# Graph attention layer on one core: k's low half kept beside zeros, tile 1 of seven heads transposed by DMA, low halves and copies recorded one step later

## The chip, the core and the metric

The kernel runs on one core of a Trainium2 chip. A core has five engines that work side by side, each through its own list of instructions in order: TensorE (PE, matrix products, with its weight loads PEld), VectorE (DVE), ScalarE (ACT), GpSimd (POOL) and SyncE (SP). SP computes nothing here; it issues most DMA transfers, in order, and one that waits holds up those behind it. The engines tell each other through semaphores. The matrix unit reads from SBUF, 128 partitions of on-chip memory, and writes into PSUM, eight banks of 128x512 floats. The metric is the time of one execution in microseconds. Before the change three runs gave 286.29, 286.67 and 287.81 us, so the median is 286.67.

## What is computed

Input x has 384 rows (nodes) of 1024 features. With H = 16 heads of width 64, cut to what matters:

```
h    = relu(layernorm(x))
q, k, v = h @ wq.T + bq, h @ wk.T + bk, h @ wv.T + bv
q2, k2, v2 = q @ wiq.T + biq, k @ wik.T + bik, v @ wiv.T + biv     # per head 384 x 64
mask = -inf, and softplus(edge weight of its type) where an edge is; the diagonal filled
attn = softmax(q2 @ k2.T / 8 + mask)                              # 16 heads, 384 x 384
y    = x + (attn @ v2) @ wo.T + bo
```

The products are kept close to float32 by splitting every operand into a high half (rounded to the type that PE reads fast) and a low half (what the rounding left). A product then takes three matmuls: high by high, high by low, low by high.

## The kernel before

**Stages.** A weight matrix comes in 8 chunks of 128x1024. A chunk is loaded by SP (`load`, line 70), its high half is made by ACT (`split_hi`, lines 90 and 94) and its low half by DVE or POOL (`split_lo`, lines 101 and 103). `mm3` (lines 432 to 435) issues the three matmuls of a product. The first 150 us hold the layer norm, the projections v and q, the product iv, the projection k, and on POOL and DVE the mask: 51 indirect DMAs of POOL write edge values into tables in DRAM (line 290), which come back and are merged into the tile `ma`. In that stage `extra_v(m)` does POOL and DVE work of the mask after chunk m of v, and `residual` loads the output bias into a tile named `bot`.

**The attention loop.** From about 150 us on, one loop of 60 steps i (line 945) interleaves everything that is left, and this hand-written order sets the order on every engine. A tile i = 3h + t is rows t*128 to t*128+127 of the scores of head h. A pair p is two heads, 2p and 2p+1, whose q and k rows come from one chunk each of wiq and wik.

- Step i: PE makes the scores of tile i (`do_S`, line 844), two matmuls of 384 columns. DVE adds the mask and takes the row minimum of tile i-1 (`do_ttr`, line 850), ACT takes the exponential of tile i-2 (line 854), DVE the reciprocal of the row sum of tile i-3 (line 867). There are two PSUM banks for scores, so the scores of tile i can only be written when DVE has read tile i-2.
- The probabilities have to be transposed before they meet v2. Tile t = 0 goes by DMA: DVE scales the reciprocal (line 869), ACT writes the high half (`do_high`, line 877) into a plane buffer, a step later DVE writes the low half (`do_low`, line 881) and SP issues a DMA transpose of both (`do_turn`, line 885). Tiles t = 1 and 2 go through PE: POOL multiplies by the reciprocal (line 871), PE does three 128x128 transposes per tile (`turn_mm`, line 891) in step 3h+7, a step later ACT (line 898) and DVE (line 899) copy high and low halves out of PSUM (`do_pt`). Three plane buffers lie in a spare part of the tile `pt`.
- Every six steps, `av_mm` (line 909) multiplies a pair's transposed probabilities with v2, 18 matmuls.
- Between those, `fill` gives out the matmuls of the q2 and k2 chunks (`fill_qk`) and later of the output product (`fill_o`), about 2.6 products of three matmuls per step. It runs ahead: 28 products are given out before step 0 (PRE), and a pair's chunks end about five steps before its first scores.
- `qk_head(w)` runs when chunk w begins, every three steps. It evacuates the chunk before (`qk_done`), makes the high half of chunk w+2, and loads chunk w+5. A function put into the list `later` runs in the next step, right after that step's `do_ttr`.

**q2 and k2 of a pair** (`qk_done`). `evac` writes the high half by ACT (line 443) and the low half by DVE (line 444) into the tile `nat`. For q, four copies by DMA put high and low half of a head above each other (64 rows each) into the tile `qs`. For k, four copies of 64 rows put high and low half of a head into both row halves of the tile `ks`. The first score matmul then multiplies q's high and low rows with k's high half, the second both with k's low half.

**Output scale.** `o_scale` (line 643) needs a maximum over all partitions: PE transposes a column (line 142), and DVE reads it in the next instructions (line 124).

Of the kernel before, what the change touches and what calls it, by code (L numbers as in the profile page):

```python
# [26 lines left out]
def gnn_kernel(ctx: ExitStack, tc: tile.TileContext, x, edges, erows, etw, wq, wk, wv, wiq, wik, wiv, wo,  # L27
# [6 lines left out]
    nc = tc.nc  # L34
# [40 lines left out]
    def split_hi(w, dst=None, dve=False):  # L75
        if w >= NCH:
            return
        if dst is None:
            t = wpool.tile([128, 2, D], F32R, tag="whl", name="whl", bufs=4)
            dst = t.rearrange("p a n -> p (a n)")  # L80
        sc = weight_scale(w)
        if sc is not None:
            dst = dst.bitcast(F16)
        whl[w] = dst[:, 0:D], dst[:, D:2 * D]
        hi = whl[w][0]
        if sc is not None:
            if dve:
                nc.vector.tensor_scalar(hi, raw[w], sc, None, op0=OP.mult)
            else:
                nc.scalar.activation(hi, raw[w], AF.Copy, scale=sc)  # L90
        elif dve:
            nc.vector.tensor_copy(hi, raw[w])
        else:
            nc.scalar.activation(hi, raw[w], AF.Copy)  # L94

    def split_lo(w, eng=None):
        if w < NCH:
            hi, lo = whl[w]
# [32 lines left out]
    def bound_of(w):  # L131
        return ((0, t_v, u_v), (1, t_iv, u_iv), (0, t_q, u_q), (1, t_iq, u_iq), (2, t_o, u_o))[BOUNDS[w]]
# [308 lines left out]

    def evac(ps, hi, lo, bias):
        nc.scalar.activation(hi, ps[:, :N], AF.Identity, bias=bias)
        nc.vector.scalar_tensor_tensor(lo, ps[:, :N], bias, hi.bitcast(F32), op0=OP.add, op1=OP.subtract)

    def evac_row(ps, hi, lo, bias):
        f = work.tile([128, N], F32, tag="e", name="f", bufs=EB)
# [49 lines left out]
    def proj(src, dst, bidx, extra=None):  # L497
        nonlocal w
        for m in range(8):
# [26 lines left out]
                extra(m)  # L526
            w += 1

    def extra_v(m):
        detect(m)  # L530

    def detect(s):

        if s == 0:
            softplus_c()
            mask_values()
        if s < NTAB:
# [14 lines left out]
    def residual(k):  # L552

        if k == 0:
            t = work.tile([128, 2, 2, N], F32R, tag="ks", name="bot")
            bob["b"] = t.bitcast(F32).rearrange("p a k n -> p (a k n)")[:, 0:D]
            nc.sync.dma_start(bob["b"], bo.partition_broadcast(128))
        if 1 <= k < 4:
            nc.sync.dma_start(xb[k - 1], x[(k - 1) * 128:k * 128, :])

    def residual_add(i):
        y = res[:, i // 2, i % 2 * 512:i % 2 * 512 + 512]
        nc.gpsimd.tensor_tensor(y, y, bob["b"][:, i % 2 * 512:i % 2 * 512 + 512], OP.add)

    nde = [0]

# [74 lines left out]
            nc.vector.tensor_scalar(ma[:, j, :], ma[:, j, :], u_c, -3.0e38, op0=OP.mult, op1=OP.max)  # L641

    def o_scale():
        bound(W0 + 5)
        nc.vector.tensor_tensor(t_out, t_out, t_o, OP.mult)

    def v2_evac(i):
        t, h = divmod(i, 2)
# [33 lines left out]
    def qk_done(w):  # L682
        n, p = chunks[w]
        q2 = nc.scalar if p == 0 else nc.sync
        nat = work.tile([128, 2, N], F32R, tag="nat", name="nat", bufs=2)
        evac(gps[w], nat[:, 0, :], nat[:, 1, :], bias_q[:, p:p + 1] if n == "iq" else bc[:, 32 + p:33 + p])
        nf = nat.bitcast(F32)
        if n == "iq":
            qs = work.tile([128, 2, N], F32R, tag="qs", name="qs")
            qf = qs.bitcast(F32)  # L690
            copies = [(nc.sync, qf[0:64, 0, :], nf[0:64, 0, :]), (q2, qf[64:128, 0, :], nf[0:64, 1, :]),
                      (nc.sync, qf[0:64, 1, :], nf[64:128, 1, :]), (q2, qf[64:128, 1, :], nf[64:128, 0, :])]
            stacks["q", p] = qs
        else:
            ks = work.tile([128, 2, 2, N], F32R, tag="ks", name="ks")
            kf = ks.bitcast(F32)
            copies = [(q2 if r else nc.sync, kf[r * 64:(r + 1) * 64, o, :, :], nf[o * 64:(o + 1) * 64, :, :])
                      for o in range(2) for r in range(2)]
            stacks["k", p] = ks
        for q, a, b in copies:  # L700
            issue = lambda q=q, a=a, b=b: q.dma_start(a, b)
            if q is nc.scalar:
                issues.append(issue)
            else:
                issue()

    tasks, later = [], []

# [10 lines left out]
    def qk_head(w):  # L719
        if pendq:  # L720
            pendq.pop(0)()
        if 0 < w - W0 < NTAB:
            mask_select(w - W0)
        split_hi(w + 2)
        while issues:
            issues.pop(0)()
        eng = nc.gpsimd if (w + 2) % 2 == PAR else None
        if w + 2 >= WO:
            later.append(lambda: later.append(lambda: split_lo(w + 2)))
        elif eng is None and now[0] >= 0:  # L730
            later.append(lambda: split_lo(w + 2))
        else:
            split_lo(w + 2, eng)
        load(w + 5)
        scan_sum(w)
        if w == W0:
            mask_select(0)
        if w == W0 + NTAB - 1:
            mask_scale()
        bound_max(w)  # L740
        if w == W0 + 6:
            o_scale()
# [64 lines left out]
    def fill_o():  # L807
# [15 lines left out]
        while todo:  # L823
# [8 lines left out]
            omm(*OT[a], k)  # L832
            yield 4

    st_ps, es, sts, tps, avs, aof = {}, {}, {}, {}, {}, {}
    S = 48

    def do_S(i):
        h, t = divmod(i, 3)
        p, o = divmod(h, 2)  # L840
        qs, ks = stacks["q", p], stacks["k", p]
        ps = st_ps[i] = bank("s")
        for s in range(2):
            nc.tensor.matmul(ps[:, :N], qs[:, o, t * 128:(t + 1) * 128], ks[:, o, s, :], start=(s == 0), stop=(s == 1))  # L844

    def do_ttr(i):
        t = i % 3
# [7 lines left out]

    ptv, plv = [], []

    def pt_setup():
        for _ in range(2):
            f = work.tile([128, 2, NT, N], F32, tag="pt", name="pt").rearrange("p a k n -> p (a k n)").bitcast(F16)  # L860
            ptv.extend(f[:, j * 6 * N:(j + 1) * 6 * N].rearrange("p (c n) -> p c n", c=6) for j in range(2))
        f = ptv.pop()
        plv.extend(f[:, 2 * j:2 * j + 2, :] for j in range(3))

    def do_norm(i):
        s = sts[i]
        nc.vector.reciprocal(s[:, 2:3], s[:, 1:2])  # L867
        if i % 3 in DT:
            nc.vector.tensor_scalar(s[:, 2:3], s[:, 2:3], PSC, None, op0=OP.mult)
        else:  # L870
            nc.gpsimd.tensor_tensor(es[i], es[i], s[:, 2:3].to_broadcast([128, N]), OP.mult)  # L871

    planes = {}

    def do_high(i):
        planes[i] = plv[i // 3 % 3]
        nc.scalar.activation(planes[i][:, 0, :], es[i], AF.Copy, scale=sts[i][:, 2:3])  # L877

    def do_low(i):
# [59 lines left out]
    t_at, a_at = {}, {}  # L939
    for h in range(16):  # L940
        for t in (1, 2):
            t_at.setdefault(3 * h + 7 if h < 15 else 3 * h + 5 + t, []).append(3 * h + t)
        if h % 2:
            a_at[3 * h + 10 if h < 15 else 3 * h + 9] = h // 2
    for i in range(S + 12):
        now[0] = i
        r = RATE if len(gens) == 2 else RATE_O if i < S else RATE_E
        fill(r / 2)
        if i < S:
            do_S(i)  # L950
        fill(r / 2)
        if 0 <= i - 1 < S:
            do_ttr(i - 1)
        run_later()
        if 0 <= i - 4 < S and (i - 4) % 3 in DT:
            do_low(i - 4)
        if 0 <= i - 2 < S:
            do_exp(i - 2)
        if 0 <= i - 3 < S:
            do_norm(i - 3)  # L960
            if (i - 3) % 3 in DT:
# [12 lines left out]
        if 0 <= i - 4 < S and (i - 4) % 3 in DT:  # L974
# [64 lines left out]
```

## Time and profile before

| what | value |
|---|---|
| median of three runs | 286.67 us |
| the profiled execution | 286.41 us |
| its span from first to last instruction | 284.7 us |
| granted TensorE clock | 0.999 |
| PE busy | 278.8 us (98%) |
| DVE busy | 214.3 us (75%) |
| ACT busy | 195.4 us (69%) |
| POOL busy | 142.5 us (50%) |
| DMA moved | 66.67 MB |
| transposes on PE | 96 |
| DMA transposes | 16 |
| copies into ks | 32 of 192 KB |

How to read it: the profile shows one execution. The 1.7 us between its time and its span lie outside the recorded instructions. A group's line in the tables gives line, engine, operation, tile written <- tiles read, shape, count, then busy time and mean length of one, then the engine's idle time just before and what ended it. Matmuls overlap each other in the array, so the length of one is not what it adds; what it adds is the distance from its start to the start of the next.

### The profile page before, as it was taken

How to read it: one execution, taken by the hardware profiler on the slowest of the kernel's cores; microseconds unless marked ns; L12 is line 12 of the kernel's file. 1: busy time of each engine (PE TensorE's matmuls, PEld its weight loads, DVE VectorE, ACT ScalarE, POOL GpSimd, SP SyncE). 2: the span in 40 equal slices, each digit the busy share in tenths (PEclk: the TensorE clock that was granted, in tenths of full speed). 3: DMA queues.
4: the chain of work that ended last, by engine and by line, in shares of the span. 5: the costliest groups of instructions: out<-in, count | busy, mean ns of one | idle time of the engine just before them, and what ended most of it. 6: DMA issues, size and time to landing. Idle time of an engine off the chain costs nothing.

```text
span 284.7 us, 5105 instructions
## 1 busy us (share of the span) xinstructions
PE 278.8 (98%) x1663; PEld 222.4 (78%) x1663; DVE 214.3 (75%) x534; ACT 195.4 (69%) x379; POOL 142.5 (50%) x148
## 2 busy tenths in 40 slices
PE   7899999999999999999999999999999999999995
PEld 6899999999954447999977897878878786556543
DVE  4868955885869654999989677878778589989524
ACT  3796878796989644228985675978787778867410
POOL 3767546457688777896003352635545332324310
PEclk9999999999999999999999999999999999999999
DMA  6899999998768931489956989896989999921106
GB/s 239 290 315 406 384 390 347 319 363 344 248 213 307 330 120 55 148 301 339 376 195 168 281 221 207 246 235 165 220 153 233 222 175 244 213 79 28 30 0 221
DMA packets 36618, 66.67 MB, mean 234 GB/s; under 512 B 17776, under 2 KB 21360, under 8 KB 36592
## 3 DMA queue, kind: packets, MB, share of 16 engines
q1 hardware_dynamic: 34208, 63.96, 73.5%
q0 software_dynamic: 2064, 1.80, 2.3%
q10 hardware_dynamic: 320, 0.59, 0.8%
q8 instruction: 13, 0.21, 0.3%
q14 instruction: 13, 0.11, 0.1%
HBM read 50.36 MB, written 3.39 MB: 189 GB/s over the span
## 4 chain that ended last, share of the span: by engine, by line
PE 95%; DMA 2%; DVE 1%; SPq 0%; issue 0%
PE g L433 23%; PE g L435 22%; PE g L434 22%; PE s L844 6%; PE a L909 4%; PE t L891 4%; DMA g<-in_x_dram 2%; PE s L433 2%; PE s L434 2%; PE s L435 2%; PE g L508 2%; PE t L435 2%; PE t L434 2%; PE t L433 2%; PE a L434 1%; PE a L433 1%
## 5 line engine op out<-in xcount | busy, mean ns | idle before, releaser
L433 PE MATMUL g<-g,whl 128*128 128x384 f32 (+1 forms) x312 | 105.4, 338 | 0.0
L435 PE MATMUL g<-g,whl 128*128 128x384 f32 (+1 forms) x312 | 103.8, 333 | 0.0
L434 PE MATMUL g<-g,whl 128*128 128x384 f32 (+1 forms) x312 | 103.8, 333 | 0.0
L290 POOL DMA_INDIRECT tab<-edge x51 | 59.6, 1168 | 32.2 <-DMA tab<-edge 14.6
L433 PEld LDWEIGHTS g<-g,whl 128*128 128x128 f32 x248 | 46.6, 188 | 0.4
L434 PEld LDWEIGHTS g<-g,whl 128*128 128x128 f32 x248 | 46.6, 188 | 0.0
L435 PEld LDWEIGHTS g<-g,whl 128*128 128x128 f32 x248 | 46.5, 188 | 0.0
L871 POOL TENSOR_TENSOR e<-e,s 128x384 f32<-128x384 f32 x32 | 26.3, 827 | 36.9 <-DVE s L867 24.1
L850 DVE CUSTOM_DVE_ANT_0 e<-s,ma,small 128x384 f32<-128x384 f32 x48 | 29.4, 612 | 10.4 <-PE s L844 8.0
L103 DVE TENSOR_TENSOR whl<-raw,whl 128x1024 fp32r<-128x1024 f32 x23 | 30.8, 1338 | 7.5 <-ACT whl L94 6.8
L94 ACT ACTIVATE whl<-raw 128x1024 fp32r<-128x1024 f32 x31 | 32.5, 1048 | 3.4 <-PE g L435 2.5
L103 POOL TENSOR_TENSOR whl<-raw,whl 128x1024 fp32r<-128x1024 f32 x8 | 19.3, 2411 | 25.2 <-ACT whl L94 18.5
L101 DVE SCALAR_TENSOR_TENSOR whl<-raw,small,whl 128x1024 f16<-128x1024 f32 x21 | 27.4, 1306 | 3.4 <-ACT whl L90 3.2
L854 ACT ACTIVATE e<-e,s 128x384 f32<-128x384 f32 x48 | 29.0, 605 | 0.7 <-DVE s L850 0.7
L844 PE MATMUL s<-ks,qs 128*128 128x384 f32 x96 | 28.9, 382 | 0.0
L90 ACT ACTIVATE whl<-raw,small 128x1024 f16<-128x1024 f32 x21 | 23.9, 1138 | 4.0 <-PE g L435 4.0
L877 ACT ACTIVATE pt<-e,s 128x384 f16<-128x384 f32 x16 | 9.8, 616 | 19.3 <-issue 12.4
L918 POOL TENSOR_TENSOR g<-aof,g 128x384 f16<-128x384 f32 x8 | 8.5, 1062 | 28.6 <-ACT g L917 28.6
L844 PEld LDWEIGHTS s<-ks,qs 128*128 128x128 f32 x96 | 17.3, 189 | 2.8 <-DVE s L850 0.2
L433 PEld LDWEIGHTS <-g 128*128 128x128 f16 x100 | 9.8, 98 | 11.7 <-issue 3.1
L435 PEld LDWEIGHTS <-g 128*128 128x128 f16 x100 | 9.8, 98 | 10.9
L899 DVE SCALAR_TENSOR_TENSOR pt<-t,pt 128x384 f16<-128x384 f32 x32 | 16.3, 550 | 1.3 <-ACT pt L898 1.2
(175 smaller groups left out, 509.5 us busy)
## 6 DMA issues: line engine op xcount, KB each, us to landing
ks<-nat SPq DMA_DIRECT2D x30, 192.0 KB
raw<-in_wv_dram SPq DMA_DIRECT2D x8, 512.0 KB
raw<-in_wq_dram SPq DMA_DIRECT2D x8, 512.0 KB
scan<-in_wiv_dram SPq DMA_DIRECT2D x8, 512.0 KB
raw<-in_wiv_dram SPq DMA_DIRECT2D x8, 512.0 KB
scan<-in_wiq_dram SPq DMA_DIRECT2D x8, 512.0 KB
raw<-in_wk_dram SPq DMA_DIRECT2D x8, 512.0 KB
raw<-in_wiq_dram SPq DMA_DIRECT2D x8, 512.0 KB
```

The costliest lines, as they stand in the source:

```text
L90: nc.scalar.activation(hi, raw[w], AF.Copy, scale=sc)
L94: nc.scalar.activation(hi, raw[w], AF.Copy)
L101: nc.vector.scalar_tensor_tensor(lo, raw[w], sc, hi, op0=OP.mult, op1=OP.subtract)
L103: (eng or nc.vector).tensor_tensor(lo, raw[w], hi.bitcast(F32), OP.subtract)
L290: nc.gpsimd.indirect_dma_start(out=tabs[c // RNG], out_offset=bass.IndirectOffsetOnAxis(ap=idx[:, c:c + 1], axis=0), in_=val[:, c:c + 1], ...
L433: nc.tensor.matmul(ps, lhi, rhi, start=first, stop=False)
L434: nc.tensor.matmul(ps, lhi, rlo, start=False, stop=False)
L435: nc.tensor.matmul(ps, llo, rhi, start=False, stop=last)
L844: nc.tensor.matmul(ps[:, :N], qs[:, o, t * 128:(t + 1) * 128], ks[:, o, s, :], start=(s == 0), stop=(s == 1))
L850: nc.vector.tensor_tensor_reduce(e, st_ps.pop(i)[:, :N], ma[:, t, :], neg_c, 3.0e38, OP.add, OP.min, s[:, 0:1])
L854: nc.scalar.activation(es[i], es[i], AF.Exp, bias=s[:, 0:1], scale=-1.0, accum_out=s[:, 1:2])
L871: nc.gpsimd.tensor_tensor(es[i], es[i], s[:, 2:3].to_broadcast([128, N]), OP.mult)
```

## The change

It has these parts.

1. **k's low half.** A new tile `kz` holds two slots (by the pair's parity) of 128 rows x 2 heads x 384. POOL writes zeros once, during stage v, into the rows of each head that are not its high q rows. For each pair DVE now writes k's low half straight from PSUM into `kz`, in two instructions of 64 rows instead of one of 128. The second score matmul reads `kz` instead of the second plane of `ks`. It therefore multiplies only q's high rows with k's low half; the product of the two low halves is left out. The copies into `ks` carry the high half alone, 96 KB each instead of 192.
2. **Tile 1 by DMA.** `in_dma(i)` says that tile 1 of heads 0, 2, 4, 6, 8, 14 and 15 goes by DMA as tile 0 does. There is a fourth plane buffer, `pl`, and planes are taken in turn.
3. **A step later.** In the loop, `evac`'s low half on DVE and the copies on SP go into `later`. `o_scale` is cut in two: the PE transpose stays, DVE's part goes into `later`. The low halves that POOL makes of the wik chunks are cut into four pieces of 256 columns, one per step.
4. **The output bias** is loaded in two halves into two smaller tiles.

```diff
+    def lo_pieces(w, c=0):
+        if w < NCH and c < D:
+            hi, lo = (a[:, c:c + D // 4] for a in whl[w])
+            nc.gpsimd.tensor_tensor(lo, raw[w][:, c:c + D // 4], hi.bitcast(F32), OP.subtract)
+            later.append(lambda: lo_pieces(w, c + D // 4))
...
     def evac(ps, hi, lo, bias):
         nc.scalar.activation(hi, ps[:, :N], AF.Identity, bias=bias)
-        nc.vector.scalar_tensor_tensor(lo, ps[:, :N], bias, hi.bitcast(F32), op0=OP.add, op1=OP.subtract)
+        if lo is not None:
+            after(lambda: nc.vector.scalar_tensor_tensor(lo, ps[:, :N], bias, hi.bitcast(F32), op0=OP.add,
+                                                         op1=OP.subtract))
+
+    def after(f):
+        if now[0] < 0:
+            f()
+        else:
+            later.append(f)
...
+    kz = work.tile([128, 2, 2, N], F32R, tag="kz", name="kz", bufs=1)
     def extra_v(m):
+        if m in (3, 4):
+            nc.gpsimd.memset(kz.bitcast(F32)[64 * (m - 3):64 * (m - 3) + 64, :, 4 - m, :], 0.0)
...
     def o_scale():
-        bound(W0 + 5)
-        nc.vector.tensor_tensor(t_out, t_out, t_o, OP.mult)
+        _, t, u = bound_of(W0 + 5)
+        ps = bank("g")
+        nc.tensor.transpose(ps[:, :128], t.to_broadcast([128, 128]), ident)
+        def rest():
+            power(t, u, ps[:, :128])
+            nc.vector.tensor_tensor(t_out, t_out, t_o, OP.mult)
+        later.append(rest)
...
-            ks = work.tile([128, 2, 2, N], F32R, tag="ks", name="ks")
+            kh = work.tile([128, 2, N], F32R, tag="nat", name="nat", bufs=2)[:, 0, :]
+            kl = kz[:, p % 2]
+            evac(gps[w], kh, None, bc[:, 32 + p:33 + p])
+            for o in range(2):
+                r = slice(o * 64, o * 64 + 64)
+                after(lambda r=r, o=o, ps=gps[w]: nc.vector.scalar_tensor_tensor(
+                    kl[r, o, :], ps[r, :N], bc[r, 32 + p:33 + p], kh.bitcast(F32)[r, :], op0=OP.add, op1=OP.subtract))
+            nf = kh.bitcast(F32)
+            ks = work.tile([128, 2, N], F32R, tag="ks", name="ks")
...
             if q is nc.scalar:
                 issues.append(issue)
             else:
-                issue()
+                after(issue)
...
+        elif now[0] >= 0:
+            lo_pieces(w + 2)
...
+    def in_dma(i):
+        h, t = divmod(i, 3)
+        return t == 0 or t == 1 and (h % 2 == 0 and h < 10 or h > 13)
...
-        for s in range(2):
-            nc.tensor.matmul(ps[:, :N], qs[:, o, t * 128:(t + 1) * 128], ks[:, o, s, :], start=(s == 0), stop=(s == 1))
+        c = slice(t * 128, (t + 1) * 128)
+        nc.tensor.matmul(ps[:, :N], qs[:, o, c], ks[:, o, :], start=True, stop=False)
+        nc.tensor.matmul(ps[:, :N], qs[:, o, c], kl[:, o, :], start=False, stop=True)
...
+        plv.extend(work.tile([128, 2, N], F16, tag="pl", name="pl", bufs=XP) for _ in range(XP))
...
-        planes[i] = plv[i // 3 % 3]
+        planes[i] = plv[npl[0] % len(plv)]
+        npl[0] += 1
...
         for t in (1, 2):
-            t_at.setdefault(3 * h + 7 if h < 15 else 3 * h + 5 + t, []).append(3 * h + t)
+            if not in_dma(3 * h + t):
+                t_at.setdefault(3 * h + 7 if h < 15 else 3 * h + 5 + t, []).append(3 * h + t)
```

The four tests `% 3 in DT` around `do_low`, `do_norm`, `do_high` and `do_turn` become `in_dma(...)` of the same tile.

More of the change, by code (lines that the diff above doesn't have):

```diff
@@ L554, in residual @@
         if k == 0:
-            t = work.tile([128, 2, 2, N], F32R, tag="ks", name="bot")
-            bob["b"] = t.bitcast(F32).rearrange("p a k n -> p (a k n)")[:, 0:D]
-            nc.sync.dma_start(bob["b"], bo.partition_broadcast(128))
+            for j in range(2):
+                t = work.tile([128, 2, N], F32R, tag="ks", name="bot")
+                bob[j] = t.bitcast(F32).rearrange("p k n -> p (k n)")[:, 0:512]
+                nc.sync.dma_start(bob[j], bo[j * 512:(j + 1) * 512].partition_broadcast(128))
         if 1 <= k < 4:
@@ L562, in residual_add @@
         y = res[:, i // 2, i % 2 * 512:i % 2 * 512 + 512]
-        nc.gpsimd.tensor_tensor(y, y, bob["b"][:, i % 2 * 512:i % 2 * 512 + 512], OP.add)
+        nc.gpsimd.tensor_tensor(y, y, bob[i % 2], OP.add)
     nde = [0]
@@ L684, in qk_done @@
         q2 = nc.scalar if p == 0 else nc.sync
-        nat = work.tile([128, 2, N], F32R, tag="nat", name="nat", bufs=2)
-        evac(gps[w], nat[:, 0, :], nat[:, 1, :], bias_q[:, p:p + 1] if n == "iq" else bc[:, 32 + p:33 + p])
-        nf = nat.bitcast(F32)
         if n == "iq":
+            nat = work.tile([128, 2, N], F32R, tag="nat", name="nat", bufs=2)
+            evac(gps[w], nat[:, 0, :], nat[:, 1, :], bias_q[:, p:p + 1])
+            nf = nat.bitcast(F32)
             qs = work.tile([128, 2, N], F32R, tag="qs", name="qs")
@@ L694, in qk_done @@
         else:
-            ks = work.tile([128, 2, 2, N], F32R, tag="ks", name="ks")
+            kh = work.tile([128, 2, N], F32R, tag="nat", name="nat", bufs=2)[:, 0, :]
[7 more added lines that the diff above has]
+            ks = work.tile([128, 2, N], F32R, tag="ks", name="ks")
             kf = ks.bitcast(F32)
-            copies = [(q2 if r else nc.sync, kf[r * 64:(r + 1) * 64, o, :, :], nf[o * 64:(o + 1) * 64, :, :])
+            copies = [(q2 if r else nc.sync, kf[r * 64:(r + 1) * 64, o, :], nf[o * 64:(o + 1) * 64, :])
                       for o in range(2) for r in range(2)]
-            stacks["k", p] = ks
+            stacks["k", p] = ks, kl
         for q, a, b in copies:
@@ L840, in do_S @@
         p, o = divmod(h, 2)
-        qs, ks = stacks["q", p], stacks["k", p]
+        qs, (ks, kl) = stacks["q", p], stacks["k", p]
         ps = st_ps[i] = bank("s")
-        for s in range(2):
-            nc.tensor.matmul(ps[:, :N], qs[:, o, t * 128:(t + 1) * 128], ks[:, o, s, :], start=(s == 0), stop=(s == 1))
+        c = slice(t * 128, (t + 1) * 128)
+        nc.tensor.matmul(ps[:, :N], qs[:, o, c], ks[:, o, :], start=True, stop=False)
+        nc.tensor.matmul(ps[:, :N], qs[:, o, c], kl[:, o, :], start=False, stop=True)
     def do_ttr(i):
@@ L856, in gnn_kernel @@
     ptv, plv = [], []
+    XP = 1
     def pt_setup():
@@ L867, in do_norm @@
         nc.vector.reciprocal(s[:, 2:3], s[:, 1:2])
-        if i % 3 in DT:
+        if in_dma(i):
             nc.vector.tensor_scalar(s[:, 2:3], s[:, 2:3], PSC, None, op0=OP.mult)
@@ L873, in gnn_kernel @@
     planes = {}
+    npl = [0]
     def do_high(i):
-        planes[i] = plv[i // 3 % 3]
+        planes[i] = plv[npl[0] % len(plv)]
+        npl[0] += 1
         nc.scalar.activation(planes[i][:, 0, :], es[i], AF.Copy, scale=sts[i][:, 2:3])
@@ L954, in gnn_kernel @@
         run_later()
-        if 0 <= i - 4 < S and (i - 4) % 3 in DT:
+        if 0 <= i - 4 < S and in_dma(i - 4):
             do_low(i - 4)
@@ L960, in gnn_kernel @@
             do_norm(i - 3)
-            if (i - 3) % 3 in DT:
+            if in_dma(i - 3):
                 do_high(i - 3)
@@ L973, in gnn_kernel @@
         run_tasks()
-        if 0 <= i - 4 < S and (i - 4) % 3 in DT:
+        if 0 <= i - 4 < S and in_dma(i - 4):
             do_turn(i - 4)
```

## Prediction

> **What bounds the kernel now.** I read the page first: busy shares, then the chain that ended last.
>
> ```profile
> span 284.7 us, 5105 instructions
> PE 278.8 (98%) x1663; PEld 222.4 (78%) x1663; DVE 214.3 (75%) x534; ACT 195.4 (69%) x379; POOL 142.5 (50%) x148
> ...
> PE 95%; DMA 2%; DVE 1%; SPq 0%; issue 0%
> ```
>
> PE is busy 98% and carries 95% of the chain. A busy PE need not be a full one, so I asked next for what PE ever waited for:
>
> ```profile
> PE g L374 <- POOL ident masks.py:199: 1.4, 1, 1.4
> PE g L354 <- DVE g L346: 1.0, 1, 1.0
> ```
>
> Both lie in the first 11 us. Going through the matmuls' start times, from 16 us to 281 us no start is more than 0.37 us after the one before. So no stall is left on PE: what is taken from PE's list shortens the kernel, and what is taken from another engine shortens nothing. The timeline of step 19 shows what a transpose really takes, and how k's copies stand:
>
> ```profile
> 196.31 0.33 PE L435 MATMUL g<-g,whl 128*128 128x384 f16 x1
> ...
> 196.47 0.82 PE L891 MATMUL t<-ident,e 128*128 128x128 f32 x6
> ...
> 196.60 0.62 DVE L444 SCALAR_TENSOR_TENSOR nat<-g,bc,nat 128x384 fp32r<-128x384 f32 x1 [0.37 <-ACT nat L443]
> ...
> 197.22 1.65 PE L909 MATMUL a<-pt,vhl 128*64 128x384 f16 x18
> ...
> 197.49 3.12 SPq L701 DMA_DIRECT2D ks<-nat  x4
> ...
> 206.93 0.51 PE L844 MATMUL s<-ks,qs 128*128 128x384 f32 x2
> ```
>
> Columns: start, length, engine, line. Six transposes start at 196.47 and the next matmul at 197.22. Pair 4's k copies start when its low half (L444) is written, and its scores come 9.4 us later. The groups of instructions by line give the prices:
>
> ```profile
> L891 PE MATMUL t<-ident,e 128*128 128x128 f32 x96 | 13.2, 272 | 0.0
> L444 DVE SCALAR_TENSOR_TENSOR nat<-g,bc,nat 128x384 fp32r<-128x384 f32 x8 | 4.9, 616 | 3.9 <-ACT nat L443 3.9
> L899 DVE SCALAR_TENSOR_TENSOR pt<-t,pt 128x384 f16<-128x384 f32 x32 | 16.3, 550 | 1.3 <-ACT pt L898 1.2
> L881 DVE SCALAR_TENSOR_TENSOR pt<-e,s,pt 128x384 f16<-128x384 f32 x16 | 10.6, 664 | 1.2 <-ACT pt L877 0.6
> L877 ACT ACTIVATE pt<-e,s 128x384 f16<-128x384 f32 x16 | 9.8, 616 | 19.3 <-issue 12.4 <-ACT e L854 4.1 <-DVE s L869 2.8
> ```
>
> **The change part by part.** The two lists of PE are equal, but for 21 transposes that are gone; kz in place of half of ks leaves the second score matmul its size.
>
> *Tile 1 of seven heads by DMA.* PE loses 7x3 transposes. In the chain, six take 0.66 us and three 0.33 us (starts 0.109 us apart), so 7x0.33 = 2.3 us, all on the path. The group's mean of 0.272 us is the length of one that overlaps its neighbours: 21x0.272 = 5.7 us is the other end (rival D). I take 2.3, because the start distances are what adds up on a dense engine. The Trainium skill ("TensorE: Matmul & The Clock Gate", Part 4: PE-mode transpose) gives about 275 ns for a transpose inside a kernel; by that the time would be 280.6. The trace agrees with that number as a length (0.272), and not as a distance.
> The rest of this part is beside PE: on DVE seven low halves (0.66) and seven small scalings (0.15, L869) come and seven of L899 (0.55) go, +1.8 us; on ACT seven of L877 (0.62) for seven of L898 (0.48), +1.0 us, with some 1.2 us of idling before each (19.3 over 16); POOL loses seven of L871 (0.83), -5.8 us; SP issues seven more transposes of 1.23 us.
>
> *k's low half.* DVE does 16 instructions of 64 rows instead of 8 of 128. No row has 64 partitions. If time goes by rows, each is half of 0.62 and nothing changes; if by the 384 columns, each is 0.62 and DVE gets +5.0 us. I take the second, nearest in columns and source. DVE thus goes from 214.3 to about 221 us; its idle quarter hides that, and if the cover went the price is up to 6.8 us (rival B). The two memsets cost POOL 2x0.73 us (1.1 us for 1152 columns, scaled to 768) near 42 us, where its scatters wait for DMA and DVE anyway (2.7 us idle before the scatter at 58.3). Were they to delay everything behind them, the mask tables would land at 138.6 instead of 137.1, and DVE first merges one at 148.4: nothing. The copies are halved: 3072-byte packets took 568 us of DMA engine time and the 1536-byte ones of as many q copies 276, so 292/16 = 18 us of all engines go; a transpose takes 23.75 us of engine time, so seven bring 10. DMA, 84 to 104% busy from 160 to 250 us, gets relief.
>
> *A step later.* Nothing is added; the question is what becomes late. DVE no longer stands waiting for ACT's high half (7.8 us of waits before L444) and reads the scores first. On SP, the copies now stand behind the load and the t = 0 transpose of the same step. The load waits for POOL's last piece or DVE's low half of an older chunk; the transpose waits for L881. For pair 5, ACT's high half ended at 209.62, POOL's split at 207.38 and L881 at 208.84. So the transpose would issue at about 208.9 and the copies at 210.1, and before they started at 210.29, held by L444. I count zero. The other end is a whole step (2.2 us) plus a transpose issue (1.23): 3.4 us late (rival C). q's copies have over 10 us to their use, and wait for the older pair's scores anyway.
>
> *POOL's pieces, o_scale, the bias.* Five chunks in four pieces cost between nothing and 4 x 0.83 - 2.41 = 0.9 us more each on an engine that is idle over half of the stage, and POOL gained 5.8. DVE's 0.9 us wait for L142 at step 7 goes. There DVE was latest: twice the scores of a tile came only 0.06 us after the bank was read (176.23 and 180.38), without PE stopping, so relief there is worth nothing in time. The two bias loads come before 110 us and are used at 118: nothing.
>
> Sum, against the profiled execution: 286.41 - 2.3 = 284.1. That execution is 0.26 us under the median of the runs shown, so a median would be 284.4; I say 284.2.
>
> **The rivals.**
>
> B. *DVE becomes late.* The scores of tile i wait for DVE's reading of tile i-2; the margin is 0.06 us at tiles 10 and 12, 0.5 to 1.0 at 9, 11 and 36, over 1.1 else. DVE gets 0.6 to 1.1 us more per pair (k's low half 0.62, each tile 1 another 0.26). For it: DVE is busy 9.66 of the 10 us from 240 on. Against: the 7.8 us of waits that go, and the AV matmuls, during which DVE catches up every six steps (0.48 us behind PE after most of them). If a sixth to a third of the 6.8 us shows at the tight places, 1.1 to 2.3 us come back: 285.2 to 286.4.
>
> C. *k's copies land too late: slower.* From the last packet of a pair's k copies to its first scores there are 1.5 us (pair 1), 1.6, 3.9, 3.4, 3.2, 3.0 and 2.1 (pair 7). At 2.5 us late, pairs 1, 2 and 7 lose 1.0+0.9+0.4 = 2.3, and the gain is gone; at 3.1 it loses 4.2 and is over 0.5% slower (288.3); at 3.4 it loses 1.9+1.8+1.3+0.2+0.4 = 5.6: 289.7. Against it: pair 5 above, and shorter transfers.
>
> D. *A transpose is worth its length:* 286.41 - 5.7 = 280.7. Against it, every start time.
>
> E. *The last AV product waits for the new transpose of head 15.* The old one issues at 263.91, after the AV product that frees its buffer, its last packet ends at 266.18, and the AV product starts at 271.05. The new one issues 1.25 us behind, so 267.5 against 270.7: 3 us spare. If another 4 us of lag came in ACT's and DVE's part, 1 us is lost: 285.1, up to 286.
>
> **How the numbers follow.** About 0.5% (1.4 us) is what a measurement can tell from no change: 285.2 to 288.1 counts as the same. Forecast 0.70 (own range 283.5 to 285.0), B 0.11, C 0.09, D 0.03, E 0.04, and 0.03 for a slower outcome that I don't see. Faster is the forecast and D, 0.73; same B and E, 0.15; slower C and the unseen, 0.12. The range holds forecast, B and E (0.85) and leaves out C, D and the unseen: 283.2 to 286.8.
>
> **What would show it.** Right: 75 transposes on PE still 0.109 apart, PE busy about 276.5 us, still no PE wait after 16 us, 23 DMA transposes; kz's instructions at 0.6 us each; k copies at or before their old distance to the scores. B would show as gaps before the score matmuls ended by DVE's row minimum, C as gaps before a pair's first scores ended by a ks transfer, E as a gap before the last AV product. The forecast is wrong if PE has gaps in the attention steps that sum to over a microsecond.

## The result and the profile after

The changed kernel takes 284.88 us (median of 16 runs, 283.96 to 286.25), the kernel before on the same chips 286.37 us (16 runs, 285.97 to 287.81). The ratio is 0.9947, with a 95% interval of 0.993 to 0.9965: 1.5 us faster, where the working had 2.3 and the forecast was 284.2 (its own range 283.5 to 285.0). Here and below, ratios and their intervals leave out executions that took over 1.5% more than the fastest of the same kernel, and medians do not, which matters for e7 to e10 alone. The profiled execution took 285.44 us, with a span of 283.6; it is 0.56 us above the median, so what is lost in it need not be lost in every execution.

The page of the changed kernel, busy shares and the chain that ended last:

```profile
span 283.6 us, 5088 instructions
PE 276.6 (98%) x1642; PEld 219.4 (77%) x1642; DVE 223.0 (79%) x549; ACT 196.1 (69%) x379; POOL 139.8 (49%) x158
...
PE 86%; DVE 5%; DMA 4%; issue 2%; SPq 1%; ACT 1%; DVEq 0%
```

PE is busy 2.2 us less, as worked out (276.5). But the chain is on PE for 86% of the span and no longer for 95%: the path now leaves PE. So the span fell by 1.1 us only. The groups by line (line, engine, operation, tile written <- read, shapes, count, then busy us and mean ns, then idle time before) hold the prices that had been forecast:

```profile
L927 DVE SCALAR_TENSOR_TENSOR pt<-e,s,pt 128x384 f16<-128x384 f32 x18 | 12.5, 694 | 1.3 <-ACT pt L923 0.4
...
L937 PE MATMUL t<-ident,e 128*128 128x128 f32 x75 | 10.8, 273 | 0.1
L726 DVE SCALAR_TENSOR_TENSOR kz<-g,bc,nat 64x384 fp32r<-64x384 f32 x16 | 9.8, 615 | 0.1
...
L927 DVE SCALAR_TENSOR_TENSOR pl<-e,s,pl 128x384 f16<-128x384 f32 x5 | 4.2, 844 | 0.4 <-ACT pl L923 0.2
```

75 transposes are left, 21 fewer. An instruction of 64 rows (L726) takes 0.615 us, as long as one of 128 rows did. One thing was not forecast: DVE is busy 223.0 us, 1.9 more than worked out (some 221). The means of L927 hide where, since they differ by buffer (0.844 into pl, 0.694 into pt) and the instructions do not: most take 0.61 or 0.62 us in either buffer, but four that start just behind one of POOL's pieces take 1.08 to 1.10, and one beside another POOL instruction takes 1.27. Those four make up about as much as the 1.9 us.

The chain of the changed kernel in order of time (start, us, what) shows where it leaves PE and what a transpose is worth:

```profile
162.08 0.61 DVE kz L726
163.12 0.59 SPq L735
163.76 3.37 DMA ks<-nat
...
177.47 0.59 SPq L735
178.11 2.67 DMA ks<-nat
180.78 0.40 PE s L884
...
190.81 0.65 PE t L937 x6
196.68 0.33 PE t L937 x3
```

Six transposes are 0.65 us of the path and three are 0.33: 0.109 each, as before. The new entries are k's copies. They carry the path at pair 1 and at pair 2. The timeline ahead of pair 1's first scores:

```profile
169.00 0.34 PE L441 MATMUL g<-g,whl 128*128 128x384 f32 x1
...
169.69 0.41 PE L884 MATMUL s<-ks,qs 128*128 128x384 f32 x1 [0.35 <-DVE s L911]
```

The starts lie 0.68 us apart; matmuls of this width otherwise start 0.17 apart, so 0.51 us is lost. The releaser named, DVE's reciprocal, is not what this instruction waits for. In the program it waits for k's and q's copies and for DVE's reading of tile 4, which ended at 167.15. The last packet of k's copies ended at 169.32. At pair 2 the last packet ended at 180.60 and the scores started at 180.76, 0.19 us late. A third new gap lies at 260.35 to 260.87: head 14's three transposes start 0.52 us after the matmul before them instead of 0.22. They need the PSUM bank that DVE empties with the first of two L945 instructions, which started at 260.18. The three gaps sum to 0.51 + 0.19 + 0.31 = 1.0 us, and 2.3 - 1.0 = 1.3 is about what the span lost (1.1).

How long k's copies stand on SP can be read from its issues at pair 5. Before:

```profile
208.68 1.23 SPq L885 DMA_TRANSPOSE pt<-pt  x1
210.29 2.78 SPq L701 DMA_DIRECT2D ks<-nat  x4
213.17 0.54 SPq L70 DMA_DIRECT2D raw<-in_wo_dram  x1
```

After:

```profile
209.32 0.36 SPq L70 DMA_DIRECT2D raw<-in_wo_dram  x1
211.52 1.22 SPq L931 DMA_TRANSPOSE pt<-pl  x1
212.83 3.02 SPq L735 DMA_DIRECT2D ks<-nat  x4
```

The prediction had the transpose at 208.9 and the copies at 210.1; they came at 211.52 and 212.83. This transpose is tile 0 of head 7, which went by DMA before the change too. It waits for more than DVE's low half: the place it writes to in `pt` still held head 4 and is freed by the AV product of pair 2, which ran on PE until 211.49. (The profile puts the wait down to a score matmul; that it is the AV product follows from the program and from these times.) In the order before, k's copies stood ahead of this transpose, which was issued at 213.81 (the one shown at 208.68 is head 6's). Now SP stood at it, and k's copies behind it.

### The profile page after: what moved, and what is told of

It reads as the page before. It is cut to its first block, busy times and chain, and to the rows that moved or that the text cites. A ratio compares the mean times of both kernels' runs of the same rounds, so it can differ in the third digit from the quotient of the medians.

```text
span 283.6 us, 5088 instructions
## 1 busy us (share of the span) xinstructions
PE 276.6 (98%) x1642; PEld 219.4 (77%) x1642; DVE 223.0 (79%) x549; ACT 196.1 (69%) x379; POOL 139.8 (49%) x158
## 4 chain that ended last, share of the span: by engine, by line
PE 86%; DVE 5%; DMA 4%; issue 2%; SPq 1%; ACT 1%; DVEq 0%
PE g L439 20%; PE g L441 20%; PE g L440 20%; PE a L955 4%; PE s L884 2%; PE t L937 2%; PE s L885 2%; DMA g<-in_x_dram 2%; DMA ks<-nat 2%; PE s L439 2%; PE s L441 2%; PE s L440 2%; PE g L522 2%; PE t L441 2%; PE t L439 2%
## 5 line engine op out<-in xcount | busy, mean ns | idle before, releaser
L296 POOL DMA_INDIRECT tab<-edge x51 | 58.9, 1154 | 31.8 <-DMA tab<-edge 16.7
L915 POOL TENSOR_TENSOR e<-e,s 128x384 f32<-128x384 f32 x25 | 20.6, 827 | 30.8 <-DVE s L911 20.6
L99 POOL TENSOR_TENSOR whl<-raw,whl 128x256 fp32r<-128x256 f32 x20 | 14.8, 757 | 15.7 <-ACT whl L94 15.7
L923 ACT ACTIVATE pt<-e,s 128x384 f16<-128x384 f32 x18 | 11.1, 616 | 14.9 <-issue 11.4
L884 PE MATMUL s<-ks,qs 128*128 128x384 f32 x48 | 20.6, 429 | 0.4 <-DVE s L911 0.3
L109 POOL TENSOR_TENSOR whl<-raw,whl 128x1024 fp32r<-128x1024 f32 x3 | 7.3, 2423 | 24.5 <-ACT whl L94 24.5
L127 ACT ACTIVATE scan<-scan 128x1024 f32<-128x1024 f32 x16 | 16.7, 1044 | 0.0
```

Source lines behind the costliest of these rows:

```text
L296: nc.gpsimd.indirect_dma_start(out=tabs[c // RNG], out_offset=bass.IndirectOffsetOnAxis(ap=idx[:, c:c + 1], axis=0), in_=val[:, c:c + 1], ...
L884: nc.tensor.matmul(ps[:, :N], qs[:, o, c], ks[:, o, :], start=True, stop=False)
```

## The experiments

A time of one execution contains 159 us ahead of the attention loop that no part of the change speeds up. Therefore the table also gives the loop: from the start of the first score matmul to the end of the last matmul of the kernel, in the profiled execution. Each loop is that of one execution; where a program was profiled twice, the two differed by 0.42 us (after and e4), 0.02 and nothing (e9, e8). In the second group of runs (e7, e8, e9, e10) times were scattered: the kernel before took 286.09 to 298.21 us there, and in the profiles of e8, e9 and e10 PE stood between 112 and 136 us in work that the edits don't touch. Of these runs the loop is read. Two of them, e8 and e9, were run again as e8b and e9b; their loops agreed (120.87 both times for e8; 122.74 and 122.76 for e9).

| kernel | tile 1 by DMA | POOL's pieces | kz | a step later | median us (before in the same group) | ratio, 95% interval | loop us |
|---|---|---|---|---|---|---|---|
| before | no | no | no | no | 286.37 | | 122.23 |
| after | yes | yes | yes | yes | 284.88 (286.37) | 0.9947, 0.993 to 0.9965 | 121.08 |
| e1 | no | yes | yes | yes | 286.16 (286.42) | 0.9979, 0.9961 to 0.9997 | 122.40 |
| e2 | yes | no | no | no | 291.64 (286.42) | 1.0171, 1.0143 to 1.0199 | 127.38 |
| e3 | yes | yes | yes | all but k's copies | 284.40 (286.42) | 0.9918, 0.9891 to 0.9944 | 120.42 |
| e4 | yes | yes | yes | as after | 284.96 (286.42) | 0.9936, 0.991 to 0.9962 | 120.66 |
| e6 | no | yes | yes | no | 286.08 (286.27) | 0.9983, 0.9965 to 1.0001 | 122.09 |
| e7 | yes | no | yes | yes | 286.20 (287.66) | 0.9955, 0.9916 to 0.9994 | 122.09 |
| e8 | yes | yes | no | no | 289.19 (287.66) | 1.0008, 0.9959 to 1.0057 | 120.87 |
| e8b | yes | yes | no | no | 285.09 (286.27) | 0.9952, 0.9929 to 0.9975 | 120.87 |
| e9 | yes | yes | yes | no | 289.78 (287.66) | 0.999, 0.9932 to 1.0048 | 122.74 |
| e9b | yes | yes | yes | no | 286.86 (286.27) | 1.0012, 0.9991 to 1.0032 | 122.76 |
| e10 | yes | yes, ao too | yes | all but k's copies | 286.55 (287.66) | 0.9914, 0.9864 to 0.9963 | 120.52 |
| e11 | yes, two heads more | yes, ao too | yes | all but k's copies | 283.41 (286.27) | 0.9894, 0.9865 to 0.9924 | 119.92 |

The theory at the outset: the 21 transposes are worth their start distance, 2.3 us, and the later copies gave back 0.7 of it. The rivals: a transpose is worth its length; the gaps are DVE's; the gain comes from the halved copies.

**e1: the transposes back on PE.**

```diff
-        return t == 0 or t == 1 and (h % 2 == 0 and h < 10 or h > 13)
+        return t == 0
```

> The changed kernel with all tile-1 transposes back on PE; the rest of the change stays. Theory (a transpose is worth its start distance of 0.109 us, and the DMA transposes themselves cause part of the new PE gaps): 2.3 us come back, and the gaps at pair 2's first scores (0.19 us) and at head 14's transposes (0.31) go, the gap at pair 1's (0.51) stays because no tile-1 transpose is issued ahead of those copies: 284.9 + 2.3 - 0.5 = 286.7. Rival 1, a transpose is worth its length of 0.272 us: 284.9 + 5.7 = 290.6. Rival 2, the transposes were beside other work and the gain came from k's halved copies: about 284.9.

286.16 us, the same as e6 and within 0.3 of before: all but 0.3 us of the gain goes with tile 1. By length it would have been 290.6. Against e3, which has no gap at pair 1 or 2, the loop is 122.40 - 120.42 = 1.98 us longer. e3 still has 0.31 us at head 14's transposes and 0.15 at tile 10, and e1 has 0.23 at pair 1; without these the 21 transposes come to 2.2 us. e8b, further down, gives the same by another way: its loop is 1.36 us shorter than before's, and it loses 0.58 us at tile 12 and 0.31 at head 14's transposes, so 2.25 without them.

**e2: tile 1 alone, put into the kernel before.**

```diff
+    def in_dma(i):
+        h, t = divmod(i, 3)
+        return t == 0 or t == 1 and (h % 2 == 0 and h < 10 or h > 13)
...
+        plv.extend(work.tile([128, 2, N], F16, tag="pl", name="pl", bufs=1) for _ in range(1))
```

> The kernel before with tile 1 of the seven heads by DMA and a fourth plane buffer, and nothing else of the change. Theory (the transposes are the whole gain, and the later copies took 0.7 us of it away): 286.4 - 2.3 = 284.1, no gap ahead of a pair's first scores, perhaps the 0.3 us at head 14's transposes: 284.1 to 284.5. Rival (the seven DMA transposes need the room that halved copies make, or push SP's copies of k back by 1.23 us each): gaps ahead of pairs' first scores, 285 or more.

291.64 us: 5.2 us slower than before, where both theories had it faster. PE's waits of e2 (engine, line waited for: us in total, times, longest) say that it is DVE, ahead of the scores:

```profile
PEld s L848 <- DVE s L854: 7.5, 7, 1.5
...
PE s L848 <- DVE s L854: 5.0, 6, 1.2
```

And its timeline says why:

```profile
195.36 1.05 ACT L94 ACTIVATE whl<-raw 128x1024 fp32r<-128x1024 f32 x1
...
196.48 2.39 POOL L103 TENSOR_TENSOR whl<-raw,whl 128x1024 fp32r<-128x1024 f32 x1 [1.68 <-ACT whl L94]
...
196.56 2.73 DVE L888 SCALAR_TENSOR_TENSOR pl<-e,s,pl 128x384 f16<-128x384 f32 x1
...
199.29 0.59 DVE L854 CUSTOM_DVE_ANT_0 e<-s,ma,small 128x384 f32<-128x384 f32 x1
...
199.94 0.62 PE L848 MATMUL s<-ks,qs 128*128 128x384 f32 x2 [0.70 <-DVE s L854]
```

Tile 1's low half on DVE starts 0.08 us after POOL's split of a wik chunk and takes 2.73 us instead of 0.62. It ends 0.42 us after POOL. This happens with all five wik chunks that POOL splits in the loop (2.66, 2.73, 2.73, 2.74 and 2.74 us), so some 10 us of DVE time are lost, the row minimum behind it comes late, and the scores of the tile after next wait.

The same was in the profile before the change, on other lines of its timeline:

```profile
148.40 1.56 DVE L303 COPY_PREDICATED ma<-mbs 128x1152 f32<-128x1152 int32 x1
149.71 2.47 POOL L103 TENSOR_TENSOR whl<-raw,whl 128x1024 fp32r<-128x1024 f32 x1 [16.84 <-ACT whl L94]
150.36 3.20 DVE L303 COPY_PREDICATED ma<-mbs 128x1152 f32<-128x1152 int32 x1
...
255.84 1.28 DVE L101 SCALAR_TENSOR_TENSOR g<-raw,small,g 128x1024 f16<-128x1024 f32 x1
...
255.91 1.98 POOL L918 TENSOR_TENSOR g<-aof,g 128x384 f16<-128x384 f32 x1 [3.11 <-ACT g L917]
...
257.03 1.27 DVE L881 SCALAR_TENSOR_TENSOR pt<-e,s,pt 128x384 f16<-128x384 f32 x1
```

The same copy takes 1.56 us where it starts ahead of POOL and 3.20 where it starts behind, and a low half takes 1.27 instead of 0.62. It goes the other way too: POOL's L918 takes 1.98 us here and 0.91 to 0.95 at its seven other places; here it started 0.07 us behind DVE's L101, whose two tensors lie in SBUF. No wait is shown: the instruction only looks long. The Trainium skill ("SBUF — State Buffer", Who interferes with whom) says that a DVE instruction with two inputs in SBUF contends with a GpSimd instruction that reads SBUF, and that the one that comes second blocks until the first is done. The traces agree. L888 reads e and a plane buffer (pt or pl) from SBUF and stood for 2.1 us; in e7's trace the row minimum and L943, which read one operand from PSUM, took their usual 0.60 and 0.55 us inside POOL's split from 181.90 to 184.31.

**e3 and e4: when k's copies are issued.** In e3 at once:

```diff
+            elif n == "ik":
+                issue()
             else:
                 after(issue)
```

and in e4, in place of that `issue()`:

```diff
+                after(lambda issue=issue: after(issue))
```

> The changed kernel, but k's copies on SP are issued at once, as before the change; low halves and q's copies stay a step later. Theory (the gaps of 0.51 and 0.19 us ahead of pair 1's and pair 2's first scores are waits for k's copies): both gaps go, 284.9 - 0.7 = 284.2, last packet to first scores 1.5 us or more at each pair. Rival 1 (they are DVE's lateness, as the list of waits names the row minimum and the reciprocal): the gaps stay, 284.9. Rival 2 (the earlier copies hold the weight loads and transposes behind them on SP): gaps elsewhere, 285 or more.

> The changed kernel with k's copies one more step later (two in all). Theory (pairs 1 and 2 already wait, and from the last packet to the first scores there are 2.5, 3.0, 2.5, 2.0 and 1.2 us at pairs 3 to 7): with some 2.2 us more, pairs 1 and 2 lose 2.2 each, pair 7 1.0, pair 6 0.2, so 284.9 + 5.6 = 290.5, with gaps of that size at those places. Rival (the copies' landing is not what the first scores wait for): no new gap, 284.9 to 285.5.

e3 took 284.40 us, and its loop is 0.66 us shorter than after's (0.24 shorter than e4's, which is the same program as after, as said below); the gap at pair 1 is gone, at pair 2 as well. From the last packet to the first scores there are now 3.0 us at pair 1 and 4.4 at pair 2, where after had 0.37 and 0.17. So the gaps at pairs 1 and 2 were waits for k's copies, and not DVE's lateness. What they cost in time is less sure: the intervals of the two ratios overlap. And with them gone another appears: the scores of tile 10 start 0.15 us late, only 0.06 us after DVE has read their bank.

e4 was an edit that did nothing. On SP only the order counts, and nothing is issued between those two places: the program is that of after, instruction by instruction. It says nothing on lateness. But it is a second execution of the same program, and there the gaps at pairs 1 and 2 are 0.1 us and none (last packets at 169.20 and 179.06, scores at 169.37 and 180.57), and tile 10's scores start 0.2 us late. After's transpose issue at 173.23 took 3.56 us, and e4's took 1.22, and the copies behind them were issued at 176.88 and 174.78. So the 0.7 us is not the same in each execution.

**e7 and e8: POOL's pieces.** e7 is after without them, e8 is e2 with them:

```diff
-        elif now[0] >= 0:
-            lo_pieces(w + 2)
```

> The changed kernel, but POOL makes each wik chunk's low half in one instruction of 1024 columns again instead of four of 256. Theory (a low half of DVE that starts while POOL is in a long split stands until POOL is done, as the 2.7 us ones of tile 1 alone did beside POOL's 2.4 us): the five low halves that now take 1.1 us take 2.7, DVE is late by up to 1.6 us five times, and part of it shows on PE: 287 to 291, with gaps ahead of score matmuls. Rival (tile 1 alone was slow because DVE stood waiting for ACT ahead of q's and k's low halves, 9.7 us, and the step later is the cure): 284.9, no new gaps.

> The kernel before with tile 1 of the seven heads by DMA and POOL's split of the wik chunks in four pieces; k's copies, low halves and the output scale as before. Theory (POOL's long instruction was what made tile 1 alone slow): DVE's low halves take 1.1 us instead of 2.7, the gaps of 1.0 to 1.6 us ahead of the scores go, 286.4 - 2.3 = 284.1, up to 285. Rival (DVE's waits for ACT are the cause): the gaps stay, 290 to 291.6.

> The kernel before with tile 1 by DMA and POOL's pieces once more, for a time: in the run before, weight loads ahead of the attention loop were late and only the loop could be read (first scores to last matmul 120.9 us, before 122.2). Theory (tile 1 and the pieces are the whole gain; kz and the later step add nothing): 286.4 - 1.4 = 285.0, as the changed kernel within 0.3. Rival (kz or the later step is needed): over 286.

e8's time can't be told from before's (ratio 1.0008), but its loop is 120.87 us; e8b took 285.09 us with the same loop. The pieces take 127.38 - 120.87 = 6.5 us off e2's loop, and with tile 1 they are the whole gain of the change: e8b is within 0.2 us of after. The same place in e8b:

```profile
191.85 1.76 POOL L99 TENSOR_TENSOR whl<-raw,whl 128x256 fp32r<-128x256 f32 x2 [1.68 <-ACT whl L94]
...
191.92 1.08 DVE L896 SCALAR_TENSOR_TENSOR pl<-e,s,pl 128x384 f16<-128x384 f32 x1
```

The low half waits for the first piece alone, and takes 1.08 us instead of 2.73.

e7 missed both theories. Its loop is 122.09, 1.0 longer than after's (1.4 longer than e4's); but its low halves do not take 2.7 us (one takes 1.07, and the rest beside wik's splits some 0.6): with q's and k's low halves a step later, DVE starts tile 1's low half some 0.46 us ahead of POOL's split and not 0.08 us behind. What is late in e7 is POOL itself:

```profile
181.90 2.41 POOL L109 TENSOR_TENSOR whl<-raw,whl 128x1024 fp32r<-128x1024 f32 x1 [4.10 <-ACT whl L94]
184.26 0.83 POOL L913 TENSOR_TENSOR e<-e,s 128x384 f32<-128x384 f32 x1
...
185.14 0.31 PEld L935 LDWEIGHTS t<-ident,e 128*128 128x128 f32 x3 [1.02 <-POOL e L913]
185.14 0.55 PE L935 MATMUL t<-ident,e 128*128 128x128 f32 x3 [0.63 <-POOL e L913]
```

The normalisation of tile 2 (L913) stands behind the long split, and PE waits for it ahead of the transposes, here 0.96 us from start to start and once more 0.67. So the pieces serve twice: DVE's low half gets in, and POOL's own next piece of work does.

**e9 and e6: nothing a step later, with and without tile 1 by DMA.** In both, q's and k's low halves and copies go out in the step of `evac`:

```diff
     def after(f):
-        if now[0] < 0:
-            f()
-        else:
-            later.append(f)
+        f()
```

> The changed kernel with nothing of q and k a step later: low halves by DVE and all copies as early as before; tile 1 by DMA, the pieces, kz and the output scale stay. Theory (the pieces alone keep DVE in time, and the later copies cost the gaps at pairs 1 and 2): no gap ahead of pair 1 and 2, DVE waits some 8 us for ACT again, 284.2 to 285.5. Rival (the step later is what keeps DVE in time): gaps ahead of score matmuls, 287 or more.

> The changed kernel with no low half or copy of q and k a step later, once more, for the same reason (loop 122.7 us with gaps of 1.2 and 0.8 ahead of scores). Theory (kz's extra instructions make DVE late where it also waits for ACT, and the later step is what pays for them): the gaps at tiles 9 to 12 show again, 286 to 286.6, loop 122 or more. Rival (the gaps came from the late start of that execution): 284.5 to 285, loop 121 or less.

> The changed kernel with tile 1 back on PE and nothing of q and k later: what stays is kz with DVE's two instructions of 64 rows, the pieces, the output scale and the bias in halves. Theory (DVE's extra 4.9 us are hidden but at the tight tiles 9 to 12): loop 122.2 to 122.8, 286.4 to 287.0. Rival (they are hidden nowhere, or the pieces help by themselves): more than 288, or under 286.

e9's time can't be told from before's (ratio 0.999). e9b took 286.86 us, 2.0 more than after and 1.8 more than e8b, which differs from it by kz and the output scale. Its PE waits again name the row minimum:

```profile
PEld s L881 <- DVE s L888: 2.6, 5, 1.3
...
PE s L881 <- DVE s L888: 1.3, 2, 0.9
```

They are the gaps at 175.88 and 181.02 (1.22 and 0.79 us from start to start), the scores of tiles 10 and 12 at the end of the stretch in which DVE is latest, in both runs. e6, which is e9 with tile 1 on PE, took 286.08, the same as before within its interval, and its loop (122.09) has no start more than 0.37 us after the one before. So kz's 4.9 us more on DVE are hidden by themselves, and tile 1's work is but for 0.6 us at tile 12 if the pieces are there (e8b), but both together are not. The later step takes 1.7 us off the loop (e9b to after), and e3 shows that k's copies are not the part that helps. That it helps by sparing DVE its waits for ACT is argued from the totals of those waits (given below), not tested by itself.

**e10 and e11: POOL's low half of ao in pieces, and two heads more.** e10 is e3 with:

```diff
-        nc.gpsimd.tensor_tensor(ao[:, 1, p, :], aof[p], ao[:, 0, p, :], OP.subtract)
+        aos_lo(p)
+    def aos_lo(p, c=0):
+        r = slice(c, c + 128)
+        nc.gpsimd.tensor_tensor(ao[:, 1, p, r], aof[p][:, r], ao[:, 0, p, r], OP.subtract)
+        if c < 256:
+            if p < 7:
+                later.append(lambda: aos_lo(p, c + 128))
+            else:
+                aos_lo(p, c + 128)
```

and e11 also has `h % 2 == 0 or h == 15` for the heads whose tile 1 goes by DMA.

> The changed kernel with k's copies at once, and POOL's low half of the attention output in three pieces of 128 columns, one per step. Theory (the gap of 0.52 us instead of 0.22 ahead of head 14's transposes is DVE being late by the low half that stood 1.27 us beside POOL's 2.0 us instruction): that low half takes about 0.9 us or less and the gap shrinks to 0.22, 284.4 - 0.3 = 284.1. Rival (the gap is due to DVE's count of instructions there): 284.4 and the gap stays.

> The changed kernel with k's copies at once, POOL's low half of the attention output in three pieces, and tile 1 of heads 10 and 12 by DMA as well (all even heads and 15). Theory (each further head takes 0.33 us from PE, and DVE's 0.26 us a head are covered there): 284.4 - 0.3 - 0.66 = 283.4. Rival (DVE, nearly full from 240 us on, becomes late): gaps ahead of scores of heads 10 to 15, 284 to 286.

In e10 the gap at head 14's transposes is gone: none of its starts in the loop is late but one at tile 10 (0.76 us apart). The low half that took 1.27 us beside POOL's 1.98 us instruction takes 0.78. The time can't be compared with e3's (other group), and the loop is no shorter than e3's (120.52 against 120.42), because tile 10's scores now lose 0.6 us where they lost 0.15. So the 0.3 us is shown by the gap alone, and DVE's lateness at tile 10 takes it back in this execution. e11 took 283.41 us against 286.27 for before, ratio 0.9894, the lowest of this study, though its interval overlaps those of e3 and e10. It has 69 transposes on PE, which is busy 275.9 us, and no scores of heads 10 to 15 start late. Its loop is 0.60 us shorter than e10's, near the 0.66 expected for six transposes. But e11's loop started at 158.0, 0.95 us earlier than after's in work that is the same in both, so a comparison of single spans flatters it; the loop and the median are what counts.

## Why the prediction was right, and where it was not

**PE is dense, and a transpose is worth 0.109 us: right.** PE lost 2.2 us of busy time, the chain has 0.33 for three, and with the gaps taken out the 21 transposes measure 2.2 us (e3 against e1). That it is worth its length (5.7 us) is refuted by e1. The Trainium skill ("TensorE: Matmul & The Clock Gate", Part 4: PE-mode transpose) gives about 275 ns: the trace has that as the length (273 ns), and the runs have 2.2/21 = 0.105 us as what one takes from the path.

**"Tile 1 by DMA ... beside PE": right in the sum, wrong as a part.** Counting instructions gave DVE 1.8 us more, hidden. By itself it cost DVE some 10 us more and the kernel 5.2 us (e2). The duration of an instruction was taken from a row in which POOL was mostly idle beside it; the new instructions fell beside POOL's long splits. It came out right because other parts of the change take that away: the pieces (e8b), and the later step (e7, where the low halves are short without them). No term of the working says so, so that was luck.

**"POOL's pieces ... between nothing and 0.9 us more each on an engine that is idle": the step that failed most.** They were priced as a small cost, with no gain looked for. The cost was right: a chunk takes 2.95 to 3.3 us in pieces and 2.41 whole. The gain was missed: 6.5 us of the loop beside tile 1 alone (e2 to e8b) and 1.0 in the full change (e7 to after). Without tile 1 by DMA it is at most 0.3 us (e6 and e1, which have the pieces beside kz).

**k's low half: right.** 16 instructions of 0.615 us, as taken (by columns, not by rows), hidden when alone (e6). In the full change it needs the later step to be hidden (e9b). The two memsets took 0.74 us each, as worked out, at 24 and 29 us and not near 42.

**"A step later ... I count zero": wrong on both sides, a gain and a loss.** With the later step DVE waits for ACT 3.2 us before L451 (5.6 in e9b, and 1.3 more before kz's instructions; 7.8 before the change), and kz and tile 1 fit together: 2.0 us (e9b to after). Without tile 1 by DMA it gains nothing (e6 and e1). Against it, k's copies came late. At pair 5 the working missed that SP stands at the transpose of head 7's tile 0 until the AV product is done (2.6 us; the copies were issued 2.7 us later than worked out). The working knew this kind of wait: under rival E it has the last transpose issue "after the AV product that frees its buffer". That did no harm at pair 5, but at pairs 1 and 2, where before only 1.5 and 1.6 us were spare, up to 0.7 us was lost. Not all of that was spare, either: it was counted to the last packet, and the scores started 0.37 and 0.17 us after it. At pair 1 there is no transpose ahead; there the copies were issued 0.7 us later and behind two weight loads instead of one, and their first packet came at 165.37 instead of 163.28.

**Rivals.** C (late copies) was the right place with a small dose: the copies landed 1.6 and 1.8 us later at pairs 1 and 2, not the 2.5 from which it would have eaten the gain. B (DVE late) did happen, but at one place not listed, head 14's transposes, for 0.3 us; at tiles 10 and 12 the margin held in after's trace, where the loss at pair 1 stands ahead of them. Where that loss is smaller or gone, tile 10's scores start late: 0.2 us in e4, 0.15 in e3, 0.6 in e10. E did not: the last transpose's packets ended at 267.11, and the AV product started at 269.81. The 0.7 us between 284.2 and 284.88 is of the size of these two, C and B.

**The signs named beforehand.** 75 transposes 0.109 us apart, 23 DMA transposes, PE's busy time and kz's 0.6 us came as said. Two signs did not: PE waits after 16 us, and k's copies land closer to the scores than before. The forecast was to be wrong if PE's gaps in the attention steps sum to over a microsecond. In after's profile they sum to 1.0 us, so it lies on that line, and was right by little.

## What to carry to other kernels

Before an instruction is added to DVE, look in the trace for DVE instructions that are far longer than their group's mean without a wait being shown, and see what POOL does beside them: two engines that look idle in the shares can still stand in each other's way, and cutting one long POOL instruction into pieces can be worth more than the work that was moved. On an engine or a queue that runs in order, ask what each instruction ahead waits for, all of its waits and not only the best known one: that, and not the step it is written in, says when a transfer is issued. Price work removed from a dense engine by the distance of starts, and then count the new gaps.

## What the runs showed that was not expected

- A DVE instruction with both tensors in SBUF that starts 0.07 to 0.15 us after a 2.4 us POOL instruction takes 2.66 to 2.74 us instead of 0.62; the profile shows it as busy and not as waiting. Cut into four, POOL's work took 0.72 to 1.11 us a piece, 2.95 to 3.6 us a chunk (after and e8b), and the DVE instruction some 1.08.
- The coincidence was no accident of one execution: in e2 POOL's split starts 1.02 to 1.03 us after the end of one and the same ACT instruction (L443), and DVE's low half 1.10 to 1.17 us after it, at all five places. In e7, with q's and k's low halves a step later, one of them met a split, and that late in it (1.07 us).
- Two executions of one and the same program (after and e4) differed by 0.4 us in the loop: 0.51 and 0.1 us were lost at pair 1, 0.19 and nothing at pair 2, nothing and 0.2 at tile 10. One of SP's transpose issues took 3.56 us in the one and 1.22 in the other.
